# Moving down sums between MLP rounds: round 0 accumulates in round 4, the last round takes two tiles from round 30

## The chip, the cores and the metric

The kernel runs on one core of a Trainium2 chip. The metric is device time in microseconds (us), the median over runs. The engines are named as the profile names them: PE (TensorE, matmuls), PEld (its weight loads), DVE (VectorE), ACT (ScalarE), POOL (GpSimd) and SP, whose queue issues nearly all the DMAs.

## What is computed

The input is x of 4 sequences, 512 tokens and 512 features, in float32. Two pre-norm blocks follow each other, each adding to its input:

```
x = x + gated_linear_attention(layernorm(x))     # 4 heads of 128, chunks of 128 tokens
x = x + geglu_mlp(layernorm(x))
# geglu_mlp, with Wg, Wu, Wd dequantised from 4-bit codes and a scale per 32 values:
gate = x @ Wg.T          # 512 -> 4096
up   = x @ Wu.T
out  = (gelu_tanh(gate) * up) @ Wd.T     # 4096 -> 512
```

The change is in the MLP only. The hidden width of 4096 is cut into 32 tiles of 128 (`MT = 32`). A down sum of a sequence is a sum over all 32 tiles, so the tiles may be summed in any groups and order.

## The kernel before

All matmuls of the MLP run on numbers split into pieces: a weight tile and an activation each exist as three tiles (hi, lo, mi), and a product is made of matmuls of piece with piece, collected in two PSUM tiles (`pa` from pieces 0 and 1, `pb` from piece 2) that DVE and ACT combine.

**Rounds.** `rounds = range(-3, 32)` gives 35 rounds, i = 0 to 34, with r = i - 3. Round i works on sequence i % 4 (`B` = 4) and on the tiles r to r+3 that lie in 0 to 31 (L783). Rounds 0, 1, 2 have 1, 2 and 3 tiles, rounds 3 to 31 have four, and rounds 32, 33 and 34 have 3, 2 and 1. Sequence 0 is worked on in rounds 0, 4, ..., 32, sequence 2 in rounds 2, 6, ..., 30, 34. A round holds the weights of its window of tiles; the window moves by one tile a round, so each weight tile serves four consecutive rounds, one of each sequence, and is then given up (L798 for gate/up, L806 for down, where one tile set serves two MLP tiles).

**One round.** The residual of the sequence, four tiles of 128 tokens, is loaded from DRAM (`residual`, L775). For each tile `gate_up` (L707) does two products of 12 matmuls each, gate and then up (L716); each is followed by ACT L722 and DVE L723. Gate goes through gelu on ACT (L727). After up, DVE multiplies (L734), and the result `i` is split in three: hi `ih` on ACT (L737), lo `il` on DVE (L739), `im` on DVE (L740). Then `down` (L745) sums all tiles of the round into eight PSUM tiles, two for each of the four groups n of 128 tokens: three matmuls for a tile and a group (L754), so 12 for a tile. All but the last tile are summed first, for groups 0 to 2 and then for group 3; then for each n the last tile is added, DVE adds the sum to the residual in two instructions (L766, L767), and SP stores it (L768) to the accumulator in DRAM or, in a sequence's last round, to the output.

**Order.** The order on each engine is the order of the program (`manual_schedule`). PSUM is one rotation of eight tiles (`fps`): each new tile takes the place of the one eight before it and waits until that is read. Attention of the last sequence is not yet finished when the MLP begins: `mlp()` is a generator, and at each `yield` one stage of attention, `behind(p)`, is put in between (L897 and L901). Round 0 runs between the last key products of attention. Its down sums are not emitted behind it: they are kept in `held` (L803) and emitted inside the first gate product of round 1 (L729).

**Loads of x.** The three pieces of normalised x of a sequence are 12 tiles of 256 KB. From round 3 on, six of the next round's are issued ahead, at the round's first tile, and the other six after the last up product (L795), all on SP. Round 1 issues six at its second tile; rounds 0 and 2 issue none ahead.

**Dequantisation.** The weights are unpacked in steps (`fields`, `masked`, `scaled`, `hi`, `lo`, `mi`, L191 to L214) that go through a queue. `unpack` (L292) emits one step at two points of every tile: after gelu, and between ACT's `ih` and DVE's `il` (two steps at each point in round 1). An `hi` step (ACT, L208) is put off to the next `unpack`, where its `lo` step (DVE, L211) follows. A new weight tile is begun only when three large homes are free.

**Homes.** SBUF tiles are given out by hand from 42 small homes (`one_k`, 128x512) and 24 large ones (`two_k`), first freed, first used again. If no small home is free, a large one is taken for it (L103).

Of the kernel before, what the change touches and what calls it, by code (L numbers as in the profile page):

```python
# [35 lines left out]
def f32(t):  # L36
    return t.bitcast(F32)
# [3 lines left out]
def tile_gated_linear_attention__then__nvfp4_geglu(  # L41
# [20 lines left out]
    B, T, D = x.shape  # L62
# [5 lines left out]
    MT = MLP // P  # L68
    MC = 4
# [53 lines left out]
    def psum(name):  # L123
        return fps.tile([P, T], F32, tag="p", name=name)
# [142 lines left out]
    def fetch():  # L267
        if waiting:
            nxt, make, which = waiting.pop(0)
            loaded.append((nxt, make(which)))  # L270
# [21 lines left out]
    def unpack(slots, upto):  # L292
        while rounding:
            rounding.pop(0)()
        for _ in range(slots):
            if len(queue) <= 2:
                more()
            if queue and queue[0][0] <= upto:
                queue.pop(0)[1]()
# [8 lines left out]
    def load(src, name):  # L308
        t = one_k.get(name)
        nc.sync.dma_start(f32(t), src)  # L310
        return t
# [41 lines left out]
    def settle():  # L353
        for then in settled:
            then()
        settled.clear()

    def turn():
        for hn, key, use in turned:
            tp = psum(f"tp_{key}")  # L360
            for k in range(KC):
                nc.tensor.transpose(tp[:, k * P : (k + 1) * P], f32(hn)[:, k * P : (k + 1) * P], ident)
            one_k.put(hn)
            use(tp)
        turned.clear()
# [327 lines left out]

    rounds = list(range(1 - MC, MT))
    jk = [(j, k) for j in range(3) for k in range(KC)]
    x3 = [[] for _ in rounds]

    def load_x(i, which):  # L700
        if i < len(rounds):
            for j, k in which:
                x3[i].append(load(h2d[i % B][j][k], f"x_{i}_{j}_{k}"))

    held = []

    def gate_up(mt, x, slots, upto, last, key):  # L707
        w3 = wgu[mt]

        def product(i):  # L710
            pa, pb = psum(f"pa_{i}_{key}"), psum(f"pb_{i}_{key}")
            for o, js in ((pa, (0, 1)), (pb, (2,))):
                for j in js:
                    for k in range(KC):
                        c = 2 * i + k // 2
                        nc.tensor.matmul(  # L716
                            o, w3[j][:, k % 2, c * P : (c + 1) * P], x[j * KC + k],
                            start=(j == js[0] and k == 0), stop=(j == js[-1] and k == KC - 1),
                        )
            settle()  # L720
            t = one_k.get(f"t{i}_{key}")
            nc.scalar.activation(f32(t), pb, AF.Copy, scale=-1.0 / ONE_E)  # L722
            nc.vector.tensor_tensor(f32(t), pa, f32(t), ALU.add)  # L723
            return t

        g = product(0)
        nc.scalar.activation(f32(g), f32(g), AF.Gelu_apprx_tanh, scale=ONE_E)  # L727
        unpack(slots, upto)
        while held:  # L729
            held.pop()()  # L730
        yield
        u = product(1)
        last()
        nc.vector.scalar_tensor_tensor(f32(u), f32(g), ONE_E, f32(u), ALU.mult, ALU.mult)  # L734
        one_k.put(g)
        ih, il, im = (one_k.get(f"i{j}_{key}") for j in range(3))
        nc.scalar.activation(ih, f32(u), AF.Copy, scale=HI)  # L737
        unpack(slots, upto)
        nc.vector.tensor_tensor(il, f32(u), f32(ih), ALU.subtract)  # L739
        nc.vector.scalar_tensor_tensor(im, f32(ih), ONE_E, f32(u), ALU.mult, ALU.subtract)  # L740
        one_k.put(u)
        yield
        return ih, il, im

    def down(ms, inter, a4, dst, key):  # L745

        pas = [psum(f"p_d{i}_{key}") for i in range(2 * NCH)]
        L = len(ms)

        def sums(n, which):  # L750
            for i in which:
                for o, js in ((pas[2 * n], (0, 1)), (pas[2 * n + 1], (2,))):
                    for j in js:
                        nc.tensor.matmul(  # L754
                            o, inter[i][j][:, n * P : (n + 1) * P], wd[ms[i] // 2][j][:, ms[i] % 2, :],
                            start=(i == 0 and j == js[0]), stop=(i == L - 1 and j == js[-1]),
                        )

        for ns in (range(NCH - 1), [NCH - 1]):
            for i in range(L - 1):  # L760
                for n in ns:
                    sums(n, [i])
        for n in range(NCH):
            sums(n, [L - 1])
            a = f32(a4[n])
            nc.vector.scalar_tensor_tensor(a, pas[2 * n], ONE_E, a, ALU.mult, ALU.add)  # L766
            nc.vector.tensor_tensor(a, a, pas[2 * n + 1], ALU.subtract)  # L767
            nc.sync.dma_start(dst[n], a)  # L768
        one_k.put(*a4)
        for i3 in inter:  # L770
            one_k.put(*i3)

    a4s = {}

    def residual(i):  # L775
        return [
            load(accd[t], f"acc_{i}_{t}") for t in range(i % B * NCH, (i % B + 1) * NCH)
        ]

    def mlp():  # L780
        for i, r in enumerate(rounds):
            ts = range(i % B * NCH, (i % B + 1) * NCH)
            ms = [m for m in range(r, r + MC) if 0 <= m < MT]  # L783
            inter = []
            a4 = a4s.pop(i) if i in a4s else residual(i)
            ahead = [0] if i >= B - 1 else [1] if i == 1 else []
            for q, mt in enumerate(ms):
                if q in ahead:
                    load_x(i + 1, jk[:6])

                def last():

                    if q == len(ms) - 1:
                        one_k.put(*x3[i])
                        load_x(i + 1, jk[len(x3[i + 1]) :] if i + 1 < len(rounds) else [])  # L795

                inter.append((yield from gate_up(mt, x3[i], 2 if i == 1 else 1, r + MC, last, f"{i}_{mt}")))
                if mt == r:  # L798
                    two_k.put(*wgu[mt])
            final = i + B >= len(rounds)  # L800
            dst = [of[t * P : (t + 1) * P, :] if final else accd[t] for t in ts]
            if i == 0:
                held.append(lambda ms=ms, inter=inter, a4=a4, dst=dst: down(ms, inter, a4, dst, "0"))  # L803
                continue
            down(ms, inter, a4, dst, f"{i}")
            if r >= 0 and r % 2 == 1:  # L806
                two_k.put(*wd[r // 2])
            yield


    with tc.manual_schedule():
# [33 lines left out]
        def first(n):  # L845
            first_norm(0, n, x0[n])
            take_roots()
            settle()
# [7 lines left out]
        for b in range(B):  # L856
            for j in range(3 * NCH):
                later = None
                if j < NCH:
                    if b == 0:  # L860

                        def between():
                            turn()
                            if j + 2 < NCH:
                                first(j + 2)

                        product_v(b, j, between)
                    else:
                        product_v(b, j)
                elif j < 2 * NCH:  # L870
                    product_q(b, j - NCH)
                else:
                    later = product_k(b, j - 2 * NCH)
                if b == B - 1:
                    if j == NCH - 1:
                        two_k.put(*wva, wvb)
                        one_k.put(bv_sb)
                    elif j == 2 * NCH - 1:
                        two_k.put(*wq)
                    elif j == 3 * NCH - 1:  # L880
                        two_k.put(*wk)
                        one_k.put(bk_sb)
                if j == 3 * NCH - 1:
                    two_k.put(*hT[b])
                behind(p)
                if later:
                    later()
                if p in (5, 7):
                    fetch()
                if p > 3 * NCH and p % 3:  # L890
                    unpack(1, MT)
                p += 1
                if b == B - 1 and j == 2 * NCH - 3:
                    load_x(0, jk)
                    a4s[0] = residual(0)
                if b == B - 1 and j == 2 * NCH + 1:
                    for _ in range(2):  # L897
                        next(blocks)
                        behind(p)
                        p += 1  # L900
# [51 lines left out]
```

## Time and profile before

| | us |
|---|---|
| median of 3 runs | 1349.43 (1349.36 to 1351.72) |
| the profiled execution | 1351.12 |
| its span, first to last instruction | 1349.4 |
| PE busy | 1319.6 |
| DVE busy | 989.2 |
| ACT busy | 488.3 |

The profile is of one execution. Its span is 1.7 us shorter than the time of that execution. A line of the order of time gives the start and the duration in us, the engine, the line of the kernel and the tiles out<-in; a bracket at the end gives the idle time of the engine just before it and what ended it. `p_d` are the PSUM tiles of the down sums, `tp_f` a transpose in PSUM of a normalised tile (`hn_f`), `x<-h` a load of x, `i` the pieces of the MLP's inner result. Names are cut at the buffer's number, so `wgu` is a weight piece of any gate/up tile.

### The profile page before, as it was taken

Reading aid. Unit: us, or ns where it says so; the run is one execution under the profiler, and the core shown is the slowest. Engines: PE = TensorE matmul, PEld = TensorE weight load, DVE = VectorE, ACT = ScalarE, POOL = GpSimd, SP = SyncE. Lnnn points to the kernel's source line nnn. Section 1 sums busy time; section 2 is a strip of 40 time slices with the busy share of each in tenths; the row PEclk is TensorE's granted clock in tenths of the full one; section 3 lists DMA queues with packets and bytes.
Section 4 is the critical chain, followed back from the end, with each engine's and each line's share of the span. In section 5 each row is a group of like instructions: output and inputs, shape, how many; then the busy total and the mean of one; then the engine's idle time right before and its main releaser. Section 6 shows DMA issues by size and latency. Waiting matters only on the chain.

```text
span 1349.4 us, 17021 instructions
## 1 busy us (share of the span) xinstructions
PE 1319.6 (98%) x5828; PEld 1047.7 (78%) x5828; DVE 989.2 (73%) x1639; ACT 488.3 (36%) x855; POOL 62.0 (5%) x78
## 2 busy tenths in 40 slices
PE   8999999979999999999999999999999999999997
PEld 5576767657788888888888888888888888888885
DVE  4576766588677777777777777777778787777656
ACT  2554545535333333333333333333333333333322
POOL 0031313110000000000000000000000000000000
PEclk9999999989999999999999999999999999999998
DMA  7033334875656565656565656565656565554446
GB/s 234 24 101 103 103 94 122 285 220 180 239 172 188 171 194 176 192 180 196 179 199 182 198 183 195 192 194 179 192 171 213 172 205 175 184 172 156 156 172 234
DMA packets 174950, 238.67 MB, mean 177 GB/s; under 512 B 15888, under 2 KB 74256, under 8 KB 174864
## 3 DMA queue, kind: packets, MB, share of 16 engines
q1 hardware_dynamic: 174160, 237.30, 54.4%
q8 instruction: 46, 0.75, 0.2%
q10 hardware_dynamic: 704, 0.28, 0.1%
q14 instruction: 40, 0.33, 0.1%
HBM read 184.05 MB, written 53.48 MB: 176 GB/s over the span
## 4 chain that ended last, share of the span: by engine, by line
PE 89%; DVE 4%; ACT 3%; DMA 2%; issue 1%; POOL 1%; SPq 0%; ACTq 0%; DVEq 0%; POOLq 0%
PE pa L716 33%; PE p_d L754 25%; PE pb L716 17%; PE pq L428 4%; PE pva L403 2%; PE pvb L410 2%; PE pk L440 1%; DMA x<-h 1%; PE yp L637 1%; PE dp L624 1%; PE sp L595 1%; PE yp L639 1%; ACT dm L577 0%; ACT L349 0%; DMA x<-in_x 0%
## 5 line engine op out<-in xcount | busy, mean ns | idle before, releaser
L716 PE MATMUL pa<-x,wgu 128*128 128x512 f32 x2048 | 509.2, 390 | 0.8 <-DMA x<-h 0.7
L716 PEld LDWEIGHTS pa<-x,wgu 128*128 128x128 f32 x2048 | 384.9, 188 | 82.1 <-DMA x<-h 2.4
L754 PE MATMUL p_d<-wd,i 128*128 128x512 f32 x1536 | 358.5, 391 | 7.4 <-ACT i L737 2.9
L754 PEld LDWEIGHTS p_d<-wd,i 128*128 128x128 f32 x1536 | 288.6, 188 | 71.7 <-ACT i L737 3.9
L722 ACT ACTIVATE t<-pb 128x512 f32<-128x512 f32 x256 | 151.2, 591 | 354.0 <-PE pb L716 351.0
L716 PE MATMUL pb<-x,wgu 128*128 128x512 f32 x1024 | 275.0, 390 | 0.6 <-DMA x<-h 0.4
L723 DVE TENSOR_TENSOR t<-pa,t 128x512 f32<-128x512 f32 x256 | 176.5, 690 | 102.3 <-ACT t L722 96.7
L716 PEld LDWEIGHTS pb<-x,wgu 128*128 128x128 f32 x1024 | 192.3, 188 | 41.7 <-DMA x<-h 1.3
L766 DVE SCALAR_TENSOR_TENSOR acc<-p_d,acc 128x512 f32<-128x512 f32 x140 | 96.0, 686 | 109.6 <-PE p_d L754 106.4
L737 ACT ACTIVATE i<-t 128x512 fp32r<-128x512 f32 x128 | 81.0, 633 | 194.7 <-DVE t L734 191.7
L727 ACT ACTIVATE t<-t 128x512 f32<-128x512 f32 x128 | 81.1, 633 | 154.7 <-DVE t L723 154.7
L767 DVE TENSOR_TENSOR acc<-acc,p_d 128x512 f32<-128x512 f32 x140 | 96.4, 688 | 14.6
L739 DVE TENSOR_TENSOR i<-t,i 128x512 fp32r<-128x512 f32 x128 | 88.1, 689 | 24.5 <-ACT i L737 23.0
L734 DVE SCALAR_TENSOR_TENSOR t<-t,t 128x512 f32<-128x512 f32 x128 | 88.6, 692 | 4.4
L740 DVE SCALAR_TENSOR_TENSOR i<-i,t 128x512 fp32r<-128x512 f32 x128 | 87.6, 685 | 0.0
L440 PE MATMUL pk<-wk,hT 128*128 128x512 f32 x128 | 57.6, 592 | 0.0
L428 PE MATMUL pq<-hT,wq 128*128 128x512 f32 x128 | 57.5, 593 | 0.0
L428 PEld LDWEIGHTS pq<-hT,wq 128*128 128x128 f32 x128 | 23.7, 190 | 23.9 <-issue 23.4
L440 PEld LDWEIGHTS pk<-wk,hT 128*128 128x128 f32 x128 | 23.5, 190 | 23.6 <-issue 23.4
L211 DVE SCALAR_TENSOR_TENSOR wgu<-wgu,w_gu 128x1024 fp32r<-128x1024 f32 x32 | 39.4, 1233 | 2.4 <-ACT wgu L208 2.4
L202 DVE SCALAR_TENSOR_TENSOR w_gu<-i_gu,sc_gu 128x1024 f32<-128x1024 f16 x32 | 39.7, 1240 | 0.0
L214 DVE TENSOR_TENSOR wgu<-wgu,wgu 128x1024 fp32r<-128x1024 f32 x32 | 39.5, 1234 | 0.0
(133 smaller groups left out, 914.1 us busy)
## 6 DMA issues: line engine op xcount, KB each, us to landing
x<-h SPq DMA_DIRECT2D x420, 256.0 KB
acc<-acc SPq DMA_DIRECT2D x264, 256.0 KB
h<-g SPq DMA_DIRECT2D x48, 256.0 KB
x<-in_x SPq DMA_DIRECT2D x16, 256.0 KB
pk_gu<-in_gate_p SPq DMA_DIRECT2D x32, 128.0 KB
sc_gu<-in_gate_s SPq DMA_DIRECT2D x64, 64.0 KB
pk_gu<-in_up_p SPq DMA_DIRECT2D x32, 128.0 KB
sc_gu<-in_up_s SPq DMA_DIRECT2D x64, 64.0 KB
```

What stands on the lines that cost most here:

```text
L428: nc.tensor.matmul(pq, f32(wq[k // 2])[:, k % 2, h * P : (h + 1) * P], f32(hT[b][k // 2])[:, k % 2, :], start=(k == 0), stop=(k == KC - 1),)
L440: nc.tensor.matmul(pk, f32(hT[b][k // 2])[:, k % 2, n * P : (n + 1) * P], f32(wk[k // 2])[:, k % 2, :], start=(k == 0), stop=(k == KC - 1),)
L716: nc.tensor.matmul(o, w3[j][:, k % 2, c * P : (c + 1) * P], x[j * KC + k], start=(j == js[0] and k == 0), stop=(j == js[-1] and k == KC - 1),)
L722: nc.scalar.activation(f32(t), pb, AF.Copy, scale=-1.0 / ONE_E)
L723: nc.vector.tensor_tensor(f32(t), pa, f32(t), ALU.add)
L727: nc.scalar.activation(f32(g), f32(g), AF.Gelu_apprx_tanh, scale=ONE_E)
L734: nc.vector.scalar_tensor_tensor(f32(u), f32(g), ONE_E, f32(u), ALU.mult, ALU.mult)
L739: nc.vector.tensor_tensor(il, f32(u), f32(ih), ALU.subtract)
L740: nc.vector.scalar_tensor_tensor(im, f32(ih), ONE_E, f32(u), ALU.mult, ALU.subtract)
L754: nc.tensor.matmul(o, inter[i][j][:, n * P : (n + 1) * P], wd[ms[i] // 2][j][:, ms[i] % 2, :], start=(i == 0 and j == js[0]), stop=(i == L ...
L766: nc.vector.scalar_tensor_tensor(a, pas[2 * n], ONE_E, a, ALU.mult, ALU.add)
L767: nc.vector.tensor_tensor(a, a, pas[2 * n + 1], ALU.subtract)
```

## The change

Three edits belong together:

- `tiles` is made a list. The last round (34) gets the last two tiles of round 30, the round before it of the same sequence: round 30 has tiles 27 and 28, round 34 tiles 29, 30 and 31. The weights of tiles from 29 on are not given up any more, since round 34 still needs them.
- Round 0 has no down sums of its own. It leaves its tile and its `i` pieces to round 4, whose `down` sums five tiles, tile 0 first. `held` is gone, and with it the four residual loads, the eight evictions and the four stores of round 0.
- `down` gets `at_end`. In the last round only the first tile is summed ahead for all groups, and the other tiles are summed group by group, each group followed by its eviction and store.

```diff
     rounds = list(range(1 - MC, MT))
+    tiles = [[m for m in range(r, r + MC) if 0 <= m < MT] for r in rounds]
+    tiles[-1] = tiles[-1 - B][2:] + tiles[-1]
+    tiles[-1 - B] = tiles[-1 - B][:2]
...
-    held = []
...
         unpack(slots, upto)
-        while held:
-            held.pop()()
         yield
...
-    def down(ms, inter, a4, dst, key):
+    def down(ms, inter, a4, dst, key, at_end):
...
+        ready = 1 if at_end else L - 1
         for ns in (range(NCH - 1), [NCH - 1]):
-            for i in range(L - 1):
+            for i in range(ready):
                 for n in ns:
                     sums(n, [i])
         for n in range(NCH):
-            sums(n, [L - 1])
+            sums(n, range(ready, L))
...
-    a4s = {}
...
-            ms = [m for m in range(r, r + MC) if 0 <= m < MT]
+            ms = tiles[i]
             inter = []
-            a4 = a4s.pop(i) if i in a4s else residual(i)
+            a4 = residual(i) if i > 0 else None
...
-                if mt == r:
+                if mt == r and mt < tiles[-1][0]:
                     two_k.put(*wgu[mt])
...
             if i == 0:
-                held.append(lambda ms=ms, inter=inter, a4=a4, dst=dst: down(ms, inter, a4, dst, "0"))
+                over = ms, inter
                 continue
-            down(ms, inter, a4, dst, f"{i}")
-            if r >= 0 and r % 2 == 1:
+            if i == B:
+                ms, inter = over[0] + ms, over[1] + inter
+            down(ms, inter, a4, dst, f"{i}", i == len(rounds) - 1)
+            if r >= 0 and r % 2 == 1 and r < tiles[-1][0]:
                 two_k.put(*wd[r // 2])
...
                     load_x(0, jk)
-                    a4s[0] = residual(0)
```

## The prediction

> **What bounds the kernel now.** I read the page first, then the waits of TensorE (PE), then the order of time at the places the diff touches: the first MLP rounds (247 to 345 us), the third-last full round (1223 to 1256 us) and the end.
>
> ```profile
> PE 1319.6 (98%) x5828; PEld 1047.7 (78%) x5828; DVE 989.2 (73%) x1639; ACT 488.3 (36%) x855; POOL 62.0 (5%) x78
> ```
>
> PE is busy 98% of the span, so the change, which moves matmuls and removes none, can only act on PE's remaining idle time and on what follows the last matmul. PE's waits (total us, times, longest):
>
> ```profile
> PE tp_f L362 <- DVE acc L766: 3.0, 1, 3.0
> PE p_d L754 <- ACT i L737: 2.9, 1, 2.9
> PE p_d L754 <- DVE dm L612: 2.1, 1, 2.1
> PE p_d L754 <- DVE t L723: 1.2, 1, 1.2
> ```
>
> Three of the four belong to the held down sums of round 0 (L729), the second to round 34. All were single events, so each is found in the order of time. The first place (start, duration, both us):
>
> ```profile
> 267.66 2.20 PE L754 MATMUL p_d<-wd,i 128*128 128x512 f32 x9
> ...
> 269.90 1.38 DVE L334 TENSOR_SCALAR hn_f<-xr,mv_f,rs_f 128x512 f32<-128x512 f32 x1
> ...
> 275.51 1.22 DVE L211 SCALAR_TENSOR_TENSOR wd<-wd,w_d 128x1024 fp32r<-128x1024 f32 x1 [0.97 <-ACT wd L208]
> 276.65 0.68 DVE L766 SCALAR_TENSOR_TENSOR acc<-p_d,acc 128x512 f32<-128x512 f32 x1
> ...
> 277.39 1.11 PE L362 MATMUL tp_f<-ident,hn_f 128*128 128x128 f32 x4 [2.97 <-DVE acc L766]
> ...
> 282.30 2.10 PE L716 MATMUL pa<-x,wgu 128*128 128x512 f32 x8
> ```
>
> The held sums fill all eight PSUM tiles; PE then cannot transpose (tp_f) before DVE has begun to empty them, and DVE gets there only at 276.65, behind dequantisation. The end:
>
> ```profile
> 1335.23 1.07 PE L716 MATMUL pb<-x,wgu 128*128 128x512 f32 x4
> ...
> 1339.16 4.89 PE L754 MATMUL p_d<-wd,i 128*128 128x512 f32 x12 [2.86 <-ACT i L737]
> ...
> 1340.71 0.69 DVE L766 SCALAR_TENSOR_TENSOR acc<-p_d,acc 128x512 f32<-128x512 f32 x1 [0.29 <-PE p_d L754]
> ...
> 1345.75 0.69 DVE L767 TENSOR_TENSOR acc<-acc,p_d 128x512 f32<-128x512 f32 x1
> ```
>
> With one tile in the last round nothing covers the chain from the last gate/up product (1336.3) through ACT and DVE to its down sums (1339.16), and DVE's four evictions (1.4 us each) set the end: 1346.44, then 2.9 us for the last store to the span's end at 1349.4.
>
> **The last round.** The unit: a product of 12 matmuls takes 2.72 us (1330.69 to 1333.41), so a tile's down sums take 2.72 us. Round 34 gets three tiles instead of one; the two come out of round 30, so 2 x 8.16 us are only moved. Let T be the end of the last gate/up product (1336.3 before). Before, 12 matmuls of down sums lie behind T, with 2.86 us of idle time and the waits for il and im. After, 36 lie behind it and 24 fewer ahead: T comes 24 x 0.227 = 5.44 us earlier. Behind T, tile 29's sums run to T+2.72; ih is ready at T+2.8, il at T+3.5, im at T+4.1 (rows before: 1339.1, 1339.83, 1340.43), so the first of four groups ends at T+4.4 and the next three, six matmuls or 1.36 us each, at T+8.5. DVE is free of im at T+4.1 and evicts one group per 1.4 us: end at about T+10.1. Before it was T+10.14. So the end is 5.4 us earlier (4.9 to 5.7: one wait for il/im more or less). The store behind it is the same.
>
> **Round 30, which gives the tiles away.** It now has two tiles, and the only cover for its last tile's chain is one tile's sums, 2.72 us. Round 33 has two tiles before and after: its 24 sums take 1323.89 to 1330.69, 6.80 us for 5.44, a loss of 1.36. Round 30 is worse, since it still dequantises tile 31's weights; the queue of dequantisation steps is unchanged up to round 30, so the same steps fall on its tile 28:
>
> ```profile
> 1236.42 0.63 ACT L737 ACTIVATE i<-t 128x512 fp32r<-128x512 f32 x1 [1.49 <-DVE t L734]
> ...
> 1236.95 1.04 ACT L208 ACTIVATE wgu<-w_gu 128x1024 fp32r<-128x1024 f32 x1
> ...
> 1238.03 1.23 DVE L211 SCALAR_TENSOR_TENSOR wgu<-wgu,w_gu 128x1024 fp32r<-128x1024 f32 x1 [1.65 <-ACT wgu L208]
> ...
> 1239.17 0.69 DVE L739 TENSOR_TENSOR i<-t,i 128x512 fp32r<-128x512 f32 x1
> ...
> 1239.78 0.68 DVE L740 SCALAR_TENSOR_TENSOR i<-i,t 128x512 fp32r<-128x512 f32 x1
> ```
>
> Before, tiles 29 and 30 stand between this and any down sum. After, tile 28 is the last: its product ends at 1234.13, tile 27's sums at 1236.85, ih lets one matmul go at 1237.1, the il matmul waits to 1239.9 and the im matmul to 1240.5, and nine follow: 1242.8. Unhindered it would be 1239.57, a loss of 3.2 us. Then the clock. The granted clock around the gap at the end of before (us, PE busy, clock, DMA share, GB/s):
>
> ```profile
> 1338.50:1339.00 0.50, 0.00 (x0) 1.00 0.61 234
> ...
> 1339.50:1340.00 0.50, 0.50 (x2) 0.50 0.00 0
> ...
> 1342.00:1342.50 0.50, 0.50 (x3) 0.50 0.00 0
> 1342.50:1343.00 0.50, 0.50 (x4) 0.84 0.00 0
> ```
>
> A gap of 2.86 us was followed by 3.4 us at half clock. The Trainium skill (TensorE: Matmul & The Clock Gate, Why this matters for your kernels) asks only that no PE gap exceed about 3 us; by that rule round 30's gap, 2.6 us and then 0.4, is free and the round costs 3.2. The row is nearer: 3.4 us at half clock cost up to 1.7, less what falls inside the gap. I take 1.0. Round 30: +4.2 us (3.0 without the clock, 5.5 with all of it and more). Its x loads for round 31 I cost at nothing: they are issued 1229.2 to 1237 and are needed from 1242.8; round 33, equally short, fed round 34 with no wait in the row. If the cover failed it would be as at round 3, where the first product took 336.58 to 343.47, 4.2 us too long. The moved dequantisation step (L214, 1.2 us of DVE) lands in round 31's first tile, three tiles before its use: nothing.
>
> **The first rounds.** Removed at round 1: 12 matmuls (2.72 us, back in round 4, where L=5 gives even more cover), eight DVE instructions of 0.69 us, four loads and four stores of 256 KB. PE then goes from 267.66 straight to tp_f, which needs hn_f, ready at 271.28: about 6 us before 277.39. On DVE the hi/lo step L385 (282.23 before) follows L211 directly, at 276.65, and the chain from there to t L723 shifts by 5.6 to 5.9 us. PE and DVE agree, so I take 5.8. From there to round 3 the waits in the trace are of PE for ACT, DVE, POOL and the x loads that follow them, and shift together. What is late next: hn_f (a 3.6 us gap, shorter than the gaps it replaces), then kw at 293.67, a wait of 2.15 us that grows by some 0.3.
>
> The homes: round 0's four residual tiles are no longer taken, but its three inter tiles are kept to round 4. Counting gets and puts along the code, the 42 small homes are lowest at t1 of round 1's second tile (3 free before); after, none is free and it takes a large one (4 free, so dequantisation, which wants 3, is not held). Homes are reused sooner: t0 of that tile takes the home of cd, which POOL reads to 293.76, so ACT's L722 waits about 0.6 us there (293.15 before), with DVE behind it and then round 1's sums. The load xr15 takes k's home, read by POOL to 295.77, not from 293.79; on SP's queue six x loads stand behind it, issued by 298.0 before and wanted by round 2 at 306.7: 2 us later they still land in time. Removing DMAs ahead of the x loads is worth nothing, since PE waits for no DMA there. Sum: -5.8 +2.7 +0.6 = -2.5 us. Bounds: -4 (no half clock after the shorter gap), 0 (the kw wait brings a new spell of half clock of 1.7 us and the rest is lost on ACT).
>
> **The sum.** -5.4 +4.2 -2.5 = -3.7 us. It is made against the profiled execution (span 1349.4; 1351.12 with what lies around it), and applied to the median of 1349.43: 1345.7. About 0.2%, 2.7 us, is what a measurement of this kernel can tell from no change.
>
> **Rivals.**
> First, 1344.0, chance 0.20: round 30's gap stays unpunished as by the page's rule (3.2), and the first rounds give 3.2 since ACT's wait is hidden: -5.4 +3.2 -3.2. For it: 2.15 us of waiting for kw went by at full clock. Against: the row of 2.86 us.
> Second, 1348.2, chance 0.24: the gain at the start is given back by round 3, which waits for x anyway, and only the end is left: -5.4 +4.2 = -1.2. For it: the critical chain runs through DVE, ACT and h/x transfers from 285 to 343. Against: those transfers begin at DVE instructions that shift too.
> Third, the other side, 1353.4, chance 0.06: at round 1 not the held sums but the ACT/DVE chain sets PE's restart. Then product 1 starts at 282.3 as before, the 12 matmuls come back in round 4 (+2.7), and the longer gap holds the clock at half for one or two more spells (+2.5): -5.4 +4.2 +5.2 = +4.0. It decides from the point where tp_f starts later than 277.4. Against it: hn_f's row ends at 271.28.
>
> **The numbers.** The likeliest case (0.50) is 1345.7, its own spread 1344.3 to 1347.2, of which 0.42 lies below 1346.7. Faster: 0.42 + 0.20 = 0.62; within: 0.08 + 0.24 = 0.32; slower 0.06. Range: all low bounds give -5.7 +3.0 -4.0 = -6.7, all high ones -4.9 +5.5 +0 = +0.6: 1342.7 to 1350.0.
>
> **What the changed profile should show.** No wait of tp_f for L766, tp_f near 271.3 and round 1's second product near 276; round 2 about 5 us earlier; the sums of round 4 60 in a row. In round 30 a PE wait for i (L739) of about 2.6 us and half clock behind it. At the end no PE wait over 0.5 us before the last sums, and about 13 us from the last gate/up product to the end. It is wrong if round 31 waits for x, if round 30's gap is near round 33's, or if round 2 is not at least 4 us earlier.

## The result, and the profile after

The changed kernel takes 1347.24 us (median of 12 runs, 1345.8 to 1348.97); the kernel before took 1351.55 (median of 12 runs, 1349.36 to 1352.37), 2.1 more than in the 3 runs that the prediction started from. The two medians lie 4.3 us apart; the ratio on record, which is used from here on, is 0.9975, with an interval of 0.9967 to 0.9982: 3.4 us less, 2.4 to 4.5. Predicted was 3.7 less, 1345.7 from the median of the 3 runs. The profiled execution took 1347.27 us, its span 1345.5, which is 3.9 below the span before.

In the changed kernel the lines have moved: gate/up matmuls are L719, ACT and DVE behind them L725 and L726, the three pieces L738, L740, L741, down matmuls L755, evictions L768 and L769. The page's line of the engines (busy us, share, instructions):

```profile
PE 1318.1 (98%) x5828; PEld 1047.1 (78%) x5828; DVE 983.8 (73%) x1631; ACT 489.0 (36%) x855; POOL 62.0 (5%) x78
```

PE issues the same 5828 matmuls. Its longest waits at the places that the change touches (total us, times, longest):

```profile
PE dp L624 <- POOL kw L607: 5.1, 4, 2.8
PE tp_f L362 <- DVE hn_f L334: 3.6, 1, 3.6
PE p_d L755 <- DVE i L740: 2.5, 2, 2.3
```

The waits of the down sums for dm and t and for ACT's `i`, and that of tp_f for L766, are gone. In their place stand one of 3.6 us for hn_f, a longer one for kw (2.8 instead of 2.1), a new one of 2.3 us for il and a small new one in round 1 (0.8 us, for kT L550). The first rounds on PE (start, duration, us):

```profile
265.52 1.08 PE L719 MATMUL pb<-x,wgu 128*128 128x512 f32 x4
270.22 0.66 PE L362 MATMUL tp_f<-ident,hn_f 128*128 128x128 f32 x4 [3.62 <-DVE hn_f L334]
...
273.31 2.09 PE L719 MATMUL pa<-x,wgu 128*128 128x512 f32 x8
...
288.64 1.94 PE L624 MATMUL dp<-v,kw 128*128 128x128 f32 x8 [2.83 <-POOL kw L607]
...
292.97 5.79 PE L755 MATMUL p_d<-wd,i 128*128 128x512 f32 x24
...
300.12 2.01 PE L719 MATMUL pa<-x,wgu 128*128 128x512 f32 x8
```

PE goes from round 1's first product straight to tp_f, 3.6 us idle, and the up product (273.31) follows 9.7 us behind the start of the first (263.59), against 17.5 before. Round 2 starts at 300.12, that is 36.5 us behind round 1's first product; before it was 306.69 - 264.81 = 41.9. At the wait for kw a part of this lead is given back. On DVE, L385 (the step that reads tp_f) follows L211 directly; before, the eight evictions of the held sums stood between the two. Before and after:

```profile
282.23 0.68 DVE L385 TENSOR_TENSOR g<-tp_f,g 128x512 fp32r<-128x512 f32 x1
```

```profile
275.53 0.68 DVE L385 TENSOR_TENSOR g<-tp_f,g 128x512 fp32r<-128x512 f32 x1
```

Behind the start of round 1's first product that is 17.4 us before and 11.9 after: a lead of 5.5 us, close to the 5.35 that are left at round 2.

Round 30, whose last tile is now tile 28:

```profile
1230.76 3.47 PE L755 MATMUL p_d<-wd,i 128*128 128x512 f32 x13
...
1233.58 1.04 ACT L208 ACTIVATE wgu<-w_gu 128x1024 fp32r<-128x1024 f32 x1
...
1234.65 1.23 DVE L211 SCALAR_TENSOR_TENSOR wgu<-wgu,w_gu 128x1024 fp32r<-128x1024 f32 x1 [1.64 <-ACT wgu L208]
1235.79 0.68 DVE L740 TENSOR_TENSOR i<-t,i 128x512 fp32r<-128x512 f32 x1
1236.39 0.68 DVE L741 SCALAR_TENSOR_TENSOR i<-i,t 128x512 fp32r<-128x512 f32 x1
...
1236.53 4.75 PE L755 MATMUL p_d<-wd,i 128*128 128x512 f32 x11 [2.31 <-DVE i L740]
...
1241.09 2.05 PE L719 MATMUL pa<-x,wgu 128*128 128x512 f32 x8
```

The 13th matmul of the down sums goes, the 14th waits for il. Between `ih` (ACT, 1233.04) and il stand the dequantisation steps L208 and L211. From the end of the last product (1230.76) to round 31 (1241.09) it takes 10.33 us for 5.44 us of matmuls. The granted clock there (us, PE busy, clock, DMA share, GB/s; 1.00 is full clock, 0.50 half clock):

```profile
1236.50:1237.50 1.00, 0.86 (x3) 1.00 0.59 219
...
1238.00:1241.00 3.00, 3.00 (x8) 0.50 0.26 90
1241.00:1241.50 0.50, 0.50 (x3) 0.86 0.66 250
```

The end:

```profile
1332.29 8.90 PE L755 MATMUL p_d<-wd,i 128*128 128x512 f32 x36
...
1336.52 0.69 DVE L768 SCALAR_TENSOR_TENSOR acc<-p_d,acc 128x512 f32<-128x512 f32 x1
...
1341.86 0.69 DVE L769 TENSOR_TENSOR acc<-acc,p_d 128x512 f32<-128x512 f32 x1
```

The down sums of round 34 run through 36 matmuls without a wait; the last eviction ends at 1342.55, 10.26 us behind the last product. Measured from the same mark (24 matmuls after the start of round 34) it was 10.31 before.

The spans of the two profiled executions differ by 1.2 us more than the change explains, and this 1.2 us is there before round 1 begins. At 188 us the changed kernel is 0.5 us later, at 198 us it is 1.2 earlier. That is in attention, where both run the same instructions: the first that the change takes away, a residual load of round 0, is issued at 238 us. The same stretch before

```profile
192.00:194.00 2.00, 2.00 (x10) 0.59 0.13 38
194.00:196.00 2.00, 2.00 (x7) 0.55 0.93 261
```

and after

```profile
192.00:194.00 2.00, 1.55 (x11) 1.00 0.00 0
194.00:196.00 2.00, 2.00 (x11) 1.00 0.82 231
```

shows why: the execution before had a spell of half clock there, the other not. (Of the executions of the runs below, e5 and e9 had it too, e2 to e4 and e6 to e8 had not.) So I count from the start of round 1's first product:

| stretch | predicted | measured |
|---|---|---|
| round 1's first product to round 2 | -5.2 (-5.8 and +0.6) | -5.35 |
| the same, to the start of round 30 | -2.5 | -2.15 |
| round 30 | +4.2 | +4.89 |
| rounds 31 to 33 | 0 | +0.08 |
| round 34 to the last eviction, for the tiles moved | -5.4 | -5.49 |
| sum | -3.7 | -2.67 |
| ahead of round 1 (not the change) | | -1.22 |

### The profile page after: what moved, and what is told of

It is laid out like the page before. It is cut to its first block, busy times and chain, and to the rows that moved or that the text cites. A ratio compares the mean times of both kernels' runs of the same rounds, so it can differ in the third digit from the quotient of the medians.

```text
span 1345.5 us, 17010 instructions
## 1 busy us (share of the span) xinstructions
PE 1318.1 (98%) x5828; PEld 1047.1 (78%) x5828; DVE 983.8 (73%) x1631; ACT 489.0 (36%) x855; POOL 62.0 (5%) x78
## 4 chain that ended last, share of the span: by engine, by line
PE 89%; DVE 4%; ACT 3%; DMA 2%; issue 1%; POOL 1%; SPq 0%; POOLq 0%; DVEq 0%; ACTq 0%
PE pa L719 33%; PE p_d L755 25%; PE pb L719 16%; PE pq L428 4%; PE pva L403 2%; PE pvb L410 2%; PE pk L440 2%; DMA x<-h 1%; PE yp L637 1%; PE sp L595 1%; PE dp L624 1%; PE yp L639 1%; DMA h<-g 1%; ACT L349 0%; ACT sq L448 0%
## 5 line engine op out<-in xcount | busy, mean ns | idle before, releaser
L719 PE MATMUL pa<-x,wgu 128*128 128x512 f32 x2048 | 509.4, 390 | 0.9 <-DMA x<-h 0.7
L719 PEld LDWEIGHTS pa<-x,wgu 128*128 128x128 f32 x2048 | 385.1, 188 | 82.3 <-DMA x<-h 2.5
L755 PE MATMUL p_d<-wd,i 128*128 128x512 f32 x1536 | 358.3, 391 | 3.7 <-DVE i L740 2.5
L755 PEld LDWEIGHTS p_d<-wd,i 128*128 128x128 f32 x1536 | 288.7, 188 | 67.2 <-DVE i L740 3.5
L725 ACT ACTIVATE t<-pb 128x512 f32<-128x512 f32 x256 | 151.3, 591 | 352.6 <-PE pb L719 350.1
L719 PE MATMUL pb<-x,wgu 128*128 128x512 f32 x1024 | 275.0, 390 | 0.6 <-DMA x<-h 0.4
L726 DVE TENSOR_TENSOR t<-pa,t 128x512 f32<-128x512 f32 x256 | 176.5, 689 | 104.4 <-ACT t L725 99.1
L719 PEld LDWEIGHTS pb<-x,wgu 128*128 128x128 f32 x1024 | 192.3, 188 | 41.8 <-DMA x<-h 1.4
L768 DVE SCALAR_TENSOR_TENSOR acc<-p_d,acc 128x512 f32<-128x512 f32 x136 | 93.3, 686 | 109.3 <-PE p_d L755 102.0
L738 ACT ACTIVATE i<-t 128x512 fp32r<-128x512 f32 x128 | 81.0, 633 | 196.3 <-DVE t L735 194.8
L740 DVE TENSOR_TENSOR i<-t,i 128x512 fp32r<-128x512 f32 x128 | 88.2, 689 | 24.1 <-ACT i L738 22.6
L769 DVE TENSOR_TENSOR acc<-acc,p_d 128x512 f32<-128x512 f32 x136 | 93.6, 688 | 15.6 <-PE pa L719 1.4
L741 DVE SCALAR_TENSOR_TENSOR i<-i,t 128x512 fp32r<-128x512 f32 x128 | 87.7, 685 | 0.2 <-DMA h<-g 0.2
L211 DVE SCALAR_TENSOR_TENSOR wgu<-wgu,w_gu 128x1024 fp32r<-128x1024 f32 x32 | 39.4, 1232 | 2.4 <-ACT wgu L208 2.4
```

The source lines that it names most:

```text
L719: nc.tensor.matmul(o, w3[j][:, k % 2, c * P : (c + 1) * P], x[j * KC + k], start=(j == js[0] and k == 0), stop=(j == js[-1] and k == KC - 1),)
L755: nc.tensor.matmul(o, inter[i][j][:, n * P : (n + 1) * P], wd[ms[i] // 2][j][:, ms[i] % 2, :], start=(i == 0 and j == js[0]), stop=(i == L ...
```

## The experiments

The theory: three terms that do not touch each other, a gain in the first rounds from round 0's sums and evictions, which no longer stand in round 1, a gain at the end from two more tiles behind the last product, and a loss at round 30, whose last chain is left with too little cover. The rivals: that one of the terms is nothing and another larger, and that the loss at round 30 is due to the short round as such. Each ratio is to the kernel before.

**e1 and e9, the parts at the end alone.** The changed kernel with round 0's sums held as before:

```diff
+        while held:
+            held.pop()()
...
-                over = ms, inter
+                held.append(lambda ms=ms, inter=inter, a4=a4, dst=dst: down(ms, inter, a4, dst, "0", False))
...
-            if i == B:
-                ms, inter = over[0] + ms, over[1] + inter
```

> Only the parts at the end: two tiles from round 30 to round 34 and the sums group by group; round 0's down sums are held and emitted in round 1 as before. Ledger theory (round 30 pays 4.9 us, of which 1.7 is half clock, the end gains 5.3): 0.4 us below before, a ratio of 0.9997. The prediction's own terms (4.2 and 5.4) give 1.2 below. Rival, the gap in round 30 costs only its 3.2 us of waiting: 2.1 us below, 0.9984. In its profile: tp_f waits for L766-type evictions as before; round 30 takes about 10.3 us from its last product to round 31.

Measured 0.9997 (0.9988 to 1.0005): 0.4 us below before. The rival's 0.9984 is out; 0.4 and 1.2 us are not told apart. The same kernel again, as e9:

> The kernel of e1 once more, for its profile, since e1's profiled execution was disturbed. Theory: the first rounds as before (round 2 starts 41.9 us behind round 1's first product, against 36.5 in the changed kernel), round 30 takes 3.3 to 4.9 us more than its 16.3 us of matmuls (with or without a spell of half clock), and behind the last gate/up product lie 10.3 us to the last eviction. Rival, that the end and the start act on each other: round 2 earlier than 41 us, or a round 30 unlike the changed kernel's.

Measured 0.9994 (0.9987 to 1.0001). PE's waits:

```profile
PE tp_f L362 <- DVE acc L772: 2.7, 1, 2.7
PE p_d L759 <- DVE i L744: 2.5, 2, 2.3
PE p_d L759 <- DVE dm L612: 2.1, 1, 2.1
```

The old waits of round 1 and the new one of round 30 stand side by side. Round 2 starts 41.7 us behind round 1's first product, round 30 takes 20.9 us for 16.3 of matmuls, 4.6 too much. The end gains 5.5, as in the changed kernel: gain and loss nearly cancel.

**e2, the part at the start alone.**

```diff
-    tiles[-1] = tiles[-1 - B][2:] + tiles[-1]
-    tiles[-1 - B] = tiles[-1 - B][:2]
...
-            down(ms, inter, a4, dst, f"{i}", i == len(rounds) - 1)
+            down(ms, inter, a4, dst, f"{i}", False)
```

> Only the part at the start: round 0's tile is summed in round 4; rounds 30 and 34 have four tiles and one as before. Ledger theory (5.0 us won by round 3, 2.7 given back in round 4, the 1.2 us by which the changed kernel led before round 1 being a matter of the execution): 2.2 us below before, 0.9984; the prediction said 2.5. Rival, that the lead of 1.2 us belongs to the change: 3.4 below. If the first rounds give nothing (x for round 3 waited for anyway): 0.0. With e1 the two parts should add up to the change.

Measured 0.9979 (0.9970 to 0.9988), 2.8 us below before. Round 2 starts 36.5 us behind round 1's first product, as in the changed kernel. "Nothing gained" is out. The interval holds 2.2 and 3.4 us, so it does not tell whether the 1.2 us belong to the change; the profile does, since they arise ahead of all that the change touches. (This one execution had gained only 1.1 us by round 30, against 2.15 in the changed kernel: at round 3 it was at half clock for 6.8 us instead of 3.4.) With e1: 0.9997 x 0.9979 = 0.9976, the change's own 0.9975. The parts add up, within intervals of about 1.2 us each way.

**e3, no dequantisation step in round 30's last chain.**

```diff
         nc.scalar.activation(ih, f32(u), AF.Copy, scale=HI)
-        unpack(slots, upto)
+        unpack(0 if key == "30_28" else slots, upto)
```

> The changed kernel, but at round 30's last tile no dequantisation step is emitted between ih and il; the lo and mi steps of tile 31's weights follow in round 31's first tile. Theory (the step on DVE between ih and il makes the gap, and the gap brings the half clock): round 30 loses 1.4 us as round 33 does, no half clock, 3.5 us below the changed kernel, about 6 below before, 0.9955. Rival, that two tiles give too little cover whatever stands in DVE: less than 1 us below the changed kernel, 0.997. Between: if the wait goes and the half clock stays, 1.8 below the changed kernel.

Measured 0.9950 (0.9936 to 0.9964): 6.8 us below before, about 3.4 below the changed kernel. Round 30:

```profile
1233.34 1.04 ACT L208 ACTIVATE wgu<-w_gu 128x1024 fp32r<-128x1024 f32 x1
1233.47 0.69 DVE L740 TENSOR_TENSOR i<-t,i 128x512 fp32r<-128x512 f32 x1 [0.70 <-ACT i L738]
...
1234.08 0.68 DVE L741 SCALAR_TENSOR_TENSOR i<-i,t 128x512 fp32r<-128x512 f32 x1
...
1234.21 3.18 PE L755 MATMUL p_d<-wd,i 128*128 128x512 f32 x11 [0.23 <-DVE i L740]
...
1237.23 1.98 PE L719 MATMUL pa<-x,wgu 128*128 128x512 f32 x8
```

DVE takes il as soon as ih is there, PE waits 0.23 us and round 31 begins at 1237.23: 17.59 us for the round, 1.3 too many, as round 33 loses. ACT's L208 still stands behind ih and delays nothing, and the clock stays full here. So it was the step on DVE, with the half clock behind its gap, and not the short round, that made most of the loss: 3.6 of 4.9 us. The rival's 0.997 lies outside the interval.

**e4, one tile moved instead of two.**

```diff
-    tiles[-1] = tiles[-1 - B][2:] + tiles[-1]
-    tiles[-1 - B] = tiles[-1 - B][:2]
+    tiles[-1] = tiles[-1 - B][3:] + tiles[-1]
+    tiles[-1 - B] = tiles[-1 - B][:3]
```

> The changed kernel, but only one tile goes from round 30 to round 34 (three and two tiles). Theory: round 30's last chain is covered by 24 matmuls (5.4 us) against il at 5.8 and im at 6.35 us, so it loses 0.7 us and no half clock; the end gains only 2.7: 1.5 us below the changed kernel, about 4.2 below before, 0.9969. Rival, that each moved tile costs and gains alike: 0.2 us gained at the end net, so 2.4 below before, 0.9982.

Measured 0.9955 (0.9942 to 0.9968), 6.1 us below before, more than either theory said. The down sums of round 30 and the start of round 31:

```profile
1235.28 8.70 PE L755 MATMUL p_d<-wd,i 128*128 128x512 f32 x36
1243.81 1.98 PE L719 MATMUL pa<-x,wgu 128*128 128x512 f32 x8
```

24 matmuls cover the chain: 8.53 us for 8.16. I had reckoned with the step L211 in the last chain; with three tiles it falls on tile 28, which is no longer the last, so the loss is 0.4 and not 0.7. At the end it gains 3.1 us and not 2.7 (20.8 us from the start of round 34 to the last eviction, of which 8.2 belong to the moved tile; before it was 15.75). With the first rounds the terms of its profile give -2.23 -3.13 +0.37 = -4.99, inside the interval (-7.8 to -4.3). One tile gains 3.1 us at the end where two gain 5.5, and loses 4.5 us less at round 30.

**e5, kw ahead of the state's decay on POOL.** The instruction of L585 is put aside as `decay` and issued here, behind kw and vb:

```diff
+        if "decay" in ch:
+            ch.pop("decay")()
         nc.vector.tensor_tensor(f32(dm), sp, f32(dm), ALU.mult)
```

> The changed kernel, with POOL's decay of the state (L585, 1.04 us) issued behind kw and vb instead of ahead of them, in every attention chunk. In the first rounds of the changed kernel PE waits 2.8 us for kw and runs 3.4 us at half clock behind it. Theory (what the removed held sums hid behind them is the kw chain on POOL): that wait falls to 1.8 us, the half clock there goes, 1.0 + 1.7 us: 2.7 us below the changed kernel, 0.9955 of before. Rival (what PE wins there it waits for x of round 3): equal to the changed kernel, 0.9975, with a longer wait for x<-h.

Measured 0.9979 (0.9973 to 0.9986): as the changed kernel, so the theory fell. The waits show where its gain went:

```profile
PE dp L627 <- POOL kw L608: 3.4, 4, 1.2
...
PE p_d L758 <- DVE g L386: 1.9, 1, 1.9
```

The longest wait for kw falls from 2.8 to 1.2 us, but round 1's down sums then wait 1.9 us for the PSUM tile of tp_f, which DVE L386 reads late. That is not the rival either, which had the time wait at round 3. The next thing late behind kw is the chain on ACT and DVE from the second tile's t to L386. (In this execution round 2 came later still, 39.1 us behind round 1's first product: half clock for 5.9 us behind tp_f brought L386 1.0 us later, and a second spell, from 297.5 us on, fell on the down sums themselves. In e8, with the same order on POOL and the same wait for L386, it was 36.5.)

This run also shows round 30 with the same wait for il and no half clock behind it. PE there, and then the clock:

```profile
1234.98 3.47 PE L758 MATMUL p_d<-wd,i 128*128 128x512 f32 x13
1240.75 3.16 PE L758 MATMUL p_d<-wd,i 128*128 128x512 f32 x11 [2.30 <-DVE i L743]
1243.75 1.52 PE L722 MATMUL pa<-x,wgu 128*128 128x512 f32 x6
```

```profile
1242.00:1243.00 1.00, 1.00 (x6) 1.00 0.00 0
1243.00:1244.00 1.00, 1.00 (x7) 1.00 0.44 150
```

From 1234.98 to 1243.75 are 8.77 us for 5.44: a loss of 3.3, against 4.9 with the half clock.

**e6, a large home for t of round 1's second tile.**

```diff
+            if i == 0 and key == "1_1":
+                kept, one_k.free[:] = list(one_k.free), []
+                t = one_k.get(f"t{i}_{key}")
+                one_k.free[:] = kept
```

> The changed kernel, but t of the gate product of round 1's second tile takes a large home, so that it does not follow cd, which POOL reads. The wait of ACT L725 for POOL L568 (0.5 us in the changed kernel) goes. Theory from the trace (round 1's sums began later than that chain, behind the half clock, and ran without a wait): no change in time, 0.9975. The prediction's term for it: 0.6 us below the changed kernel, 0.9970. The two are closer than a measurement, so the waits decide: whether round 1's sums start or end earlier.

Measured 0.9979 (0.9971 to 0.9988). The wait in the changed kernel was there as predicted:

```profile
286.62 0.60 ACT L725 ACTIVATE t<-pb 128x512 f32<-128x512 f32 x1 [0.49 <-POOL qc L568]
```

Without it L386 comes 0.4 us earlier, and round 2 starts 36.5 us behind round 1's first product, as with it. In the changed kernel the wait of 0.5 us cost nothing, since PE came later still, at half clock behind kw.

**e7, all of round 30 moved.** Round 30 is gone, and round 34 has five tiles:

```diff
-    tiles[-1] = tiles[-1 - B][2:] + tiles[-1]
-    tiles[-1 - B] = tiles[-1 - B][:2]
+    tiles[-1] = tiles[-1 - B] + tiles[-1]
+    tiles[-1 - B] = []
...
+            if not ms:
+                continue
+            to = i + 1 if i + 1 == len(rounds) or tiles[i + 1] else i + 2
```

(`to` takes the place of i + 1 in the loads of x.)

> The changed kernel, but round 30 gives all four tiles to round 34, which has five; round 30, its x and residual loads, evictions and stores are gone. Theory (the only loss of moving tiles is the uncovered chain of the round that is left short): nothing is lost at round 30; behind the last gate/up product lie 60 matmuls (13.6 us) and one eviction, so the last product ends 10.9 us earlier and the end 5.9 earlier: 5.5 us below the changed kernel, 0.9935 of before. Rival, that the saving at the end is bound by PE and not worth more than with three tiles, and that the five dequantisation steps pressed into round 31 or its x loads make a new wait: no better than e3, 0.995.

Measured 0.9943 (0.9932 to 0.9955), 7.7 us below before and 4.3 below the changed kernel. Of the 5.5 expected, 1.0 is lost in round 31, which takes 33.64 us instead of 32.64, because the dequantisation that had its place in round 30 is now late by one step:

```profile
1237.74 1.20 PE L719 MATMUL pb<-x,wgu 128*128 128x512 f32 x4 [0.70 <-DVE wgu L214]
```

The interval holds both the theory's 0.9935 and the rival's 0.995, so the profile decides: the loss at round 30 is gone, and the rival's new wait exists, but takes back only 1.0 us.

**e8, all together,** with round 29's last tile given to round 33 and two dequantisation steps at each point of round 31:

```diff
+    tiles[-2] = tiles[-2 - B][3:] + tiles[-2]
+    tiles[-2 - B] = tiles[-2 - B][:3]
...
-                inter.append((yield from gate_up(mt, x3[i], 2 if i == 1 else 1, r + MC, last, f"{i}_{mt}")))
+                inter.append((yield from gate_up(mt, x3[i], 2 if i in (1, 31) else 1, r + MC, last, f"{i}_{mt}")))
```

> All together: e7, e5's order on POOL, and round 29 gives one tile to round 33, so that round 33 has three and its last chain is covered by 24 matmuls (two dequantisation steps at each point of round 31, to be in time). Theory, terms added: 8.1 (e7 with the start) + 1.4 (round 33's wait, which falls from 1.4 to about 0.2 us) + 2.7 (e5): 12 us below before, 0.991. If e5's gain is waited away at round 3: 9.3 below, 0.993.

Measured 0.9939 (0.9927 to 0.9952), 8.2 us below before: not to be told from e7. Round 33 no longer loses anything (24.48 us for three tiles), but round 31, now with seven dequantisation steps, takes 34.19 us, 1.5 too many, and e5's part gives nothing. It has the lowest median of the runs, 1341.85 us.

## Why the prediction was right, step by step

**The first rounds.** Right in size: -5.35 for -5.2 at round 2, -2.15 for -2.5 at round 30. tp_f waits for hn_f alone, as forecast. That PE and DVE agree on 5.8 us did not hold: PE's lead at the up product was 7.8 us, DVE's at L385 5.5, and DVE's was the one that counted. In e2, e4 and e7 half clock behind tp_f kept the up product 1.6 us later than in the changed kernel; L385 still came 11.9 us behind round 1's first product, kw was ready at 25.0, and round 2 started at 36.5, as in the changed kernel. So the gain is that of the eight evictions that left DVE (276.65 to 282.23, 5.6 us, before); PE's further lead became waiting. The case that I had put at -4, no half clock behind tp_f, came about in the changed kernel and was worth nothing for that reason. No run took the evictions away alone.

Two terms inside were off and cancelled. The wait for kw grew by 0.7 and not 0.3, since PE came earlier than I had it (up product 9.7 us behind the first, predicted about 11.2), and the half clock fell behind this wait instead of behind tp_f. And the 0.6 us on ACT, seen in the trace as 0.49, was hidden (e6). In the changed kernel round 2's start is set by PE itself: from kw (288.64) on it runs without a wait, and L386, done at 294.29, is ready about 0.5 us before PE comes to the ninth down matmul (292.97 + 8 x 0.227 = 294.79), the one that waits for it elsewhere. Where the clock was full behind kw (e2, e4, e7), PE waits for L386 instead, as here in e2:

```profile
293.75 4.35 PE L753 MATMUL p_d<-wd,i 128*128 128x512 f32 x16 [0.89 <-DVE g L386]
```

The two paths end within 0.1 us of each other, which is chance; a saving on one of them alone gains nothing at round 2 (e6 on L386's, e8 on kw's). My second rival, that all is given back by round 3, is out: round 3's wait for x stayed as it was and came 5.0 us earlier.

**Round 30.** The mechanism is shown (e3), the size was low. The wait for il and im was 3.2 us, as worked out. The term that was mis-sized is the clock: I took 1.0 us and it cost 1.7, since the spell of half clock lay wholly behind the gap and none of it inside. In e5 it cost nothing. Both prices that I weighed therefore occur; the rule of the Trainium skill (TensorE: Matmul & The Clock Gate, Why this matters for your kernels), to allow no PE gap over about 3 us, read as making shorter gaps free, held in one of the four executions looked at with this gap (e5) and failed in three (the changed kernel, e6, e9).

**The end.** -5.49 for -5.4; the last eviction comes 10.26 us behind the last product, predicted about 10.1.

**The x loads of round 31** cost nothing, as predicted: no wait for x<-h at round 31.

**The sum.** The terms of the profile give -2.67, the runs -3.4 with an interval of 2.4 to 4.5 less. The prediction of -3.7 lies in that interval. It was too large by the clock term of round 30 and by 0.35 in the first rounds. Of the first rival one half came true, the hidden wait on ACT; the third is out, since tp_f started at 270.2 and not later than 277.4. That the one profiled span, 1345.5, fell on the predicted 1345.7 owes 1.2 us to half clock in attention and is chance.

## What to carry to other kernels

Work that is moved to cover a chain takes its cover away from where it came: look at the last chain of the giver, and at what else stands in it. Here one dequantisation step between two instructions on DVE, free while two more tiles of products lay behind it, cost 3.6 of the 5.5 us gained at the end, half clock included; moving the step, one tile less, or the whole round about doubled the gain. And where two engines come earlier, count the lead of the one that the next work waits for. A sum of three terms with both signs is best tested by running each part alone.

## What was not expected of the hardware

The same gap on PE, 2.3 us and a short second one, was followed by 3.4 us at half clock in three executions and by none in a fourth. The spells start on a common grid. In the changed kernel four begin at 288.82, 336.60, 1237.72 and 1343.54 us (edges worked out from the granted clock), which are 47.78, 948.90 and 1054.72 us behind the first: 14, 278 and 309 steps of 3.413 us, and a spell lasts one step, 3.41 us, or two. The spells of the kernel before at 192.37, 274.29, 342.56 and 1339.25 lie 24, 44 and 336 such steps behind the first.

Where round 30's gap falls on this grid sorts the four executions. In the changed kernel, e6 and e9 it lies in one step, in which PE is busy 0.31 or 0.32 of the time, and half clock begins with the next step. In e5 a step begins in the middle of the gap, at 1239.56, so that PE is busy 0.65 and 0.62 of the two steps, and none follows. The gap of 3.6 us ahead of tp_f is likewise cut in two in the changed kernel, e3 and e6 and goes unpunished, though it is the longer one. This reading is made from the traces afterwards; no run was built to test it, and it gives no threshold: at round 3, where PE waits for x, half clock follows steps with PE busy 0.63 to 0.75.

Executions differ by this: at 194 us the kernel before was at half clock and the changed one was not, with the same instructions, and 1.7 us lay between them behind it. That is more than half of the 2.7 us that the terms of this change come to.
